# Attention on one core: the maxima subtracted once per block of queries, the weighted sums accumulated in the result's place

## The chip, the core and the metric

The kernel runs on one core of a Trainium2 chip. The metric is device time in microseconds (us): the median of three runs, and beside it one execution that the hardware profiler recorded. An instruction is named by its engine and its line in the kernel: TensorE (PE in the profile, its weight loads PEld), VectorE (DVE), ScalarE (ACT), GpSimd (POOL) and SyncE (SP).

## What is computed

Two layers run over x of shape (2, 256, 64, 64), all in fp32. The first is attention over the 4096 pixels with 8 heads of 32 channels, a projection and a residual:

```python
qkv = jnp.einsum('oc,bchw->bohw', w_qkv, x)
q, k, v = jnp.split(qkv, 3, axis=1)
scores = jnp.einsum('bhdi,bhdj->bhij', q, k) / jnp.sqrt(jnp.asarray(d, x.dtype))
attn = jax.nn.softmax(scores, axis=-1)
out = jnp.einsum('bhij,bhdj->bhdi', attn, v)
return jnp.einsum('oc,bchw->bohw', w_proj, out.reshape(b, c, h, w)) + x
```

The second is a non-local block: two 1x1 convolutions with bias and 2x2 max pooling (g of 256 channels, phi of 64), theta of 64 channels without pooling, a softmax over the 1024 pooled pixels for each of the 4096 pixels, a weighted sum, a 1x1 convolution W, a batch norm from given statistics, and a residual.

## The kernel before, in words

The heads are taken in groups of four, so that a group's 4 x 32 channels fill the 128 partitions. There are four groups (QUAD: two images, two groups each), and `n` is a group's number. A group's 4096 queries are cut into eight blocks of 512 (`i`), and for every block the 4096 keys are gone through in 32 steps of 128 keys (`j`, the loop in `attend`). A step computes the scores of 128 keys and 512 queries for four heads, in two pairs of heads, with keys on the partitions. ScalarE takes the exponential of a pair (L551) out of a PSUM tile of two banks, and one step later `weigh` (L435) multiplies the exponentials of the previous step with v, all four heads side by side in one PSUM buffer `w`. The 32 results of a block are added up in an SBUF tile `num`: ScalarE copies the first (L448), VectorE adds the others (L450).

The softmax subtracts each query's true maximum over all keys. The maxima are computed a block ahead by a second product with queries on the partitions (`product`, L264). The generator `maxima` is moved on twice in every step (`advance(maxes)`), so two of its products follow each pair's scores. The products of heads 0 and 1 are reduced by VectorE directly (`plain`, L276). Those of heads 2 and 3 mostly go in pairs of key chunks: a product with the difference of two chunks, cut off at zero by ScalarE (`pair`, L283), is added to the product with the first chunk while VectorE reduces it (`joint`, L290). For the first block of a new group, half of the chunks are plain for all heads (L330). All these products, `w`, the projections of q, k and v and the denominators use one ring of four PSUM buffers (`scratch`).

The maximum is subtracted by TensorE. `negate` splits the negated maxima into three bf16 terms on GpSimd, TensorE transposes them, and `subtract` (L424) writes them into a pair's PSUM tile by two bf16 matmuls with a matrix of ones (L427), ahead of the scores, which add to them. This is done in every fourth step. In the three steps after it the tile is kept: the score product takes the difference between the keys of this step and those of the last, so that the sum in PSUM becomes the next step's scores. To this end the order of the keys (`keys`, L400) goes by turns through four chunks of 512 keys: within each half of the keys, step j takes chunk j % 4. The differences of chunks are made by GpSimd and held in `kd` (chunks 1-0 and 3-2, two buffers by turns over groups), `last_kd` (5-4 and 7-6) and `mid_kd` (2-1 and 6-5). For the first group they are made as k is projected (in `make`). For later groups `differences` and `between` are called from `make` and from the loop of `attend`, at steps written out by hand (L561 to L567). `kd` and `last_kd` serve the maxima too.

The denominator is summed apart (`add`, L458): GpSimd adds up the exponentials of the first pair of heads over the steps 1 to 30 (L469), and DMAs that add in flight do it for the second pair (L477). `normalize` is a generator that is moved on during the next block: another such DMA (L483), the column sums by TensorE (L495), a reciprocal on a reshaped copy, and at last GpSimd's product of `num` and the reciprocal into the image's result tile `y` (L526).

While a block is worked on, at most three projections (the next group's k and v, this group's q of two blocks ahead; `during`, `make`) are placed after steps 11, 19 and 27. Within an engine the order of the instructions is that of the program, with a few pinned behind others (`issue_after`). After the two groups of an image come `project` and `non_local`. In `non_local`, the running sum of the exponentials (L706 to L711) uses the same two buffers as `num`; the tiles called `double` (five buffers) hold pairs of exponentials in attention and theta in `non_local`.

Of the kernel before, what the change touches and what calls it, by code (L numbers as in the profile page):

```python
# [9 lines left out]
F32 = mybir.dt.float32  # L10
# [6 lines left out]
N = HH * WW  # L17
# [5 lines left out]
P = 128  # L23
NC = C // P
NB = 512
NI = N // NB
NJ = N // P
# [8 lines left out]
def conv_attention(  # L36
# [131 lines left out]
    def make(what, n, i):  # L168
        b, qd = QUAD[n]
        if (b, i) not in held:  # L170
            name = f"x_{what}_{n}_{i}"
            if attending:
                held.clear()
                to = xs.tile([P, NC, NB], F32, tag="x", name=name)
            else:
                to = single(name)
            held[b, i] = load_x(b, i, to)
        xc = held[b, i]
        name = f"{what}_{b}_{qd}_{i}"
        pq = scratch(name)  # L180
        if what == "v":
            if i == 0:
                v[n] = qkv.tile([P, NJ, QH, D], F32, tag="v", name=f"v_{n}")
            for j in range(NB // P):
                for c in range(NC):
                    nc.tensor.matmul(  # L186
                        pq[:, bass.ts(j, P)],
                        xc[:, c, bass.ts(j, P)],
                        wv_sb[:, c, bass.ts(qd, P)],
                        start=(c == 0),  # L190
                        stop=(c == NC - 1),
                    )
                if j % 2 == 1:
                    yield
            nc.scalar.copy(v[n][:, bass.ts(i, NB // P)].rearrange("p j h d -> p (j h d)"), pq)
            return
        for c in range(NC):
            nc.tensor.matmul(  # L198
                pq,
                wqk_sb[:, c, qd, 0 if what == "q" else 1, :],  # L200
                xc[:, c, :],
                start=(c == 0),
                stop=(c == NC - 1),
            )
            yield
        if what == "q":
            to = q[n, i] = qkv.tile([P, NB], F32, tag="q", name=f"q_{n}_{i}", bufs=3)
        else:
            if i == 0:
                k[n] = qkv.tile([P, N], F32, tag="k", name=f"k_{n}")  # L210
            to = k[n][:, bass.ts(i, NB)]
        nc.scalar.copy(to, pq)
        if what == "k" and i % 4 == 2 and n == 0:
            between(n, i // 4)
        if what == "k" and i % 2 == 1 and n == 0:
            if i == 1:
                kd[n] = qkv.tile([P, NI // 4, NB], F32, tag="kd", name=f"kd_{n}")
            two = k[n][:, bass.ts(i // 2, 2 * NB)]
            nc.gpsimd.tensor_sub(  # L219
                (kd[n] if i < NI // 2 else last_kd)[:, i // 2 % (NI // 4), :],  # L220
                two[:, NB:],
                two[:, :NB],
            )
        elif what == "k" and i == NI // 2 - 1:
            kd[n] = qkv.tile([P, NI // 4, NB], F32, tag="kd", name=f"kd_{n}")
            differences(n, 0, kd[n])

    last_kd = const.tile([P, NI // 4, NB], F32, name="last_kd")  # L230

    def differences(n, half, to):
        two = k[n][:, bass.ts(half, N // 2)].rearrange("p (c t n) -> p c t n", t=2, n=NB)
        nc.gpsimd.tensor_sub(to, two[:, :, 1, :], two[:, :, 0, :])


    mid_kd = const.tile([P, 2, NB], F32, name="mid_kd")

    def between(n, half):
        two = k[n][:, N // 2 * half + NB :]  # L240
        nc.gpsimd.tensor_sub(mid_kd[:, half, :], two[:, NB : 2 * NB], two[:, :NB])

# [143 lines left out]
    def attend(b, y):  # L388
        class Block:


            def __init__(self, qd, i):
                self.n, self.qd, self.i = QUAD.index((b, qd)), qd, i
                self.name = f"{b}_{qd}_{i}"
                self.rows = self.n * NI + i
                self.num = None
                self.sums = {}
                self.last = []

        def keys(j):  # L400

            return j // 16 * 16 + j % 4 * 4 + j % 16 // 4

        def score(s, pair, blk, j):

            half, c, cols = j // 16, j % 4, bass.ts(j % 16 // 4, P)
            if c == 0:
                kj = k[blk.n][:, bass.ts(keys(j), P)]
            elif c == 2:
                kj = mid_kd[:, half, cols]  # L410
            else:
                kj = (last_kd if half else kd[blk.n])[:, c // 2, cols]
            for t in range(2):
                h = 2 * pair + t
                nc.tensor.matmul(  # L415
                    s[:, t, :],
                    kj[bass.ts(h, D), :],
                    q[blk.n, blk.i][bass.ts(h, D), :],
                    start=False,
                    stop=True,  # L420
                    skip_group_check=j % 4 > 0,
                )

        def subtract(s, pair, blk):  # L424
# [10 lines left out]
        def weigh(blk, j, p):  # L435

            w = scratch(f"w_{blk.name}_{j}")
            for h in range(QH):
                nc.tensor.matmul(  # L439
                    w[bass.ts(h, D), :],  # L440
                    v[blk.n][:, keys(j), h, :],
                    p[h // 2][:, h % 2, :],
                    start=True,
                    stop=True,
                )
            if j == 0:
                blk.num = work.tile([P, NB], F32, tag="num", name=f"num_{blk.name}")
                nc.scalar.copy(blk.num, w)  # L448
            else:
                nc.vector.tensor_add(blk.num, blk.num, w)  # L450

# [27 lines left out]
        def normalize(blk):  # L479
# [43 lines left out]
                for _ in range(13):  # L523
                    yield
            with tc.issue_after(added.ins):
                nc.gpsimd.tensor_mul(y[:, blk.qd, bass.ts(blk.i, NB)], blk.num, r)  # L526

        waiting, normal = None, iter(())
        for qd in range(QUADS):
            for i in range(NI):  # L530
                blk = Block(qd, i)
                items = [x for x in during(blk.n, i) if x[1] < len(QUAD)]
                both = [None, None]
                for j in range(NJ):
                    if j % 2 == 0:
                        two = double(f"p_{blk.name}_{j}_1")
                    p = [single(f"p_{blk.name}_{j}_0"), two[:, j % 2]]
                    for pair in (1, 0):
                        if j % 4 == 0:
                            s = both[pair] = scores(f"s_{blk.name}_{j}_{pair}")  # L540
                            subtract(s, pair, blk)
                            advance(maxes)
                            score(s, pair, blk, j)
                        else:
                            s = both[pair]
                            score(s, pair, blk, j)
                            advance(maxes)
                        with ExitStack() as order:
                            if cut is not None:
                                order.enter_context(tc.issue_after(cut.ins))  # L550
                            nc.scalar.activation(p[pair], s, AF.Exp, scale=scale)  # L551
                    if waiting is not None:
                        weigh(*waiting)
                        if j == 0:
                            normal = normalize(waiting[0])
                    add(blk, j, p, two)
                    waiting = blk, j, p
                    if j == 2 or j >= AFTER:
                        advance(normal)
                    if j % 2 == 0:  # L560
                        make_rows()  # L561
                        if (i, j) == (0, 2) and blk.n > 0:
                            between(blk.n, 1)
                        if (i, j) == (0, NJ // 4) and blk.n > 0:
                            differences(blk.n, 1, last_kd)
                        if (i, j) == (NI - 1, NJ // 2 + 2) and blk.n + 1 < len(QUAD):
                            between(blk.n + 1, 0)  # L567
                    elif j % 8 == 3 and j > 8 and items:
                        advance(make(*items.pop(0)), 9)
        weigh(*waiting)  # L570
# [26 lines left out]

    def non_local(b, y, theta_w, phi_w):
        theta = [double(f"theta_{b}_{t}") for t in range(2)]
        theta = [t[:, a, c, :] for t in theta for a in range(2) for c in range(2)]  # L600

        kv = qkv.tile([P, M + NC * M + M - 2 * P], F32, tag="k", name=f"kv_{b}")
# [100 lines left out]
        def weigh(i, t, p):  # L703
            if t == 0:
                acc[i] = [scratch(f"y_{b}_{i}_0"), scratch(f"y_{b}_{i}_1")]
                acc[i].append(work.tile([P, NB], F32, tag="num", name=f"sum1_{b}_{i}"))  # L706
                nc.gpsimd.tensor_add(acc[i][NC], p[:, 0, :], p[:, 1, :])
            else:

# [149 lines left out]
```

## Time and profile before

| | us |
|---|---|
| median of three runs (lowest, highest) | 3987.23 (3986.58, 3989.69) |
| the profiled execution, its time | 3986.37 |
| its span, first to last instruction | 3984.6 |
| TensorE busy | 3949.7 |
| VectorE busy | 2937.8 |
| GpSimd busy | 2903.6 |
| ScalarE busy | 2671.5 |
| attention of the first image, first to last weighing | 103.1 to about 1774 |
| attention of the second image | 2068.4 to about 3704 |
| exponentials L551: 2048 of | 1.025 |
| adds into num, L450: 992 of | 0.687 |
| first copies into num, L448: 32 of | 0.597 |
| adds of the first pair's exponentials, L469: 945 of | 2.460 |

TensorE's granted clock was 0.997 of full speed. A line of the costliest groups reads: line, engine, operation, output and inputs by the program's names, their shapes, how often; then the group's busy time in us and the mean of one in ns; then the idle time of the engine just before them and what ended it. A line of the timeline reads: start and duration in us, engine, line, operation, output and inputs, shapes, count, and in brackets the idle time before it with what released it. An fp32 matmul shows as two records.

### The profile page before, as it was taken

The page shows a single profiled execution, that of the slowest core. Times are in us where ns is not written, and L with a number is a line of the kernel's source. Part 1 is how long each engine was busy: PE and PEld are TensorE (multiplying, and loading weights), DVE is VectorE, ACT ScalarE, POOL GpSimd, SP SyncE. Part 2 cuts the span into 40 slices and gives each one's busy share as a digit, 9 for nine tenths or more (in the row PEclk, how much of TensorE's full clock was granted, in tenths as well). Part 3 has the DMA queues.
Part 4 walks back from the last instruction along what each step waited for, and adds up shares of the span by engine and source line. Part 5 has one row for each costly group of instructions (what it writes and reads, how often), then busy time and mean ns, then how long its engine had stood idle before and what let it go on. Part 6 is the DMA issues. An engine that isn't in the chain of part 4 may idle for free.

```text
span 3984.6 us, 72269 instructions
## 1 busy us (share of the span) xinstructions
PE 3949.7 (99%) x28592; PEld 1450.9 (36%) x28592; DVE 2937.8 (74%) x5451; ACT 2671.5 (67%) x3328; POOL 2903.6 (73%) x1851
## 2 busy tenths in 40 slices
PE   8999999999999999999999999999999999999998
PEld 4333333333333333333333333333333333333333
DVE  5877877788777787774457877787888888884434
ACT  4777777777777777751137777777677777777121
POOL 1888888888888888871448888888888888886043
PEclk9999999999999999999999999999999999999999
DMA  1777877887777777880017788878787778778200
GB/s 56 146 160 165 166 165 164 170 166 163 165 162 164 163 165 164 170 198 8 22 39 163 165 166 166 173 165 170 162 173 164 164 165 166 163 163 182 66 16 27
DMA packets 113941, 569.56 MB, mean 143 GB/s; under 512 B 20296, under 2 KB 22600, under 8 KB 52416
## 3 DMA queue, kind: packets, MB, share of 16 engines
q0 software_dynamic: 68832, 501.25, 62.8%
q1 hardware_dynamic: 44080, 62.88, 4.5%
q8 instruction: 224, 3.67, 0.4%
q14 instruction: 117, 0.96, 0.1%
q10 hardware_dynamic: 688, 0.79, 0.1%
HBM read 54.78 MB, written 8.88 MB: 16 GB/s over the span
## 4 chain that ended last, share of the span: by engine, by line
PE 97%; DVE 2%; DMA 0%; ACT 0%; POOL 0%; issue 0%; DVEq 0%; ACTq 0%
PE w L439 26%; PE ps L264 26%; PE s L415 24%; PE y L715 6%; PE s L427 3%; PE q L198 2%; PE v L186 2%; PE k L198 2%; PE den L495 1%; PE g L640 1%; DVE r L729 1%; PE f L683 1%; PE proj L584 1%; PE f L749 1%; PE tp L624 0%; PE tp L620 0%
## 5 line engine op out<-in xcount | busy, mean ns | idle before, releaser
L469 POOL TENSOR_TENSOR p<-p,p 128x1024 f32<-128x1024 f32 x945 | 2324.7, 2460 | 557.0 <-ACT p L551 550.1
L551 ACT ACTIVATE p<-s 128x1024 f32<-128x1024 f32 x2048 | 2089.9, 1025 | 624.1 <-PE ps L264 408.5
L264 PE MATMUL ps<-k,q 32*128 32x512 f32 x6232 | 2049.0, 627 | 4.0 <-DVE part L276 1.7
L276 DVE TENSOR_REDUCE part<-ps 128x1 f32<-128x512 f32 x2136 | 1369.9, 686 | 574.2 <-PE ps L264 557.7
L439 PE MATMUL w<-p,v 128*32 128x512 f32 x8192 | 1091.0, 605 | 0.7 <-ACT p L551 0.7
L450 DVE TENSOR_TENSOR num<-num,w 128x512 f32<-128x512 f32 x992 | 681.4, 687 | 92.7 <-PE w L439 91.3
L290 DVE CUSTOM_DVE_ANT_0 ps<-ps,over 128x512 f32<-128x512 f32 x980 | 676.0, 693 | 32.1 <-PE ps L264 27.9
L264 PEld LDWEIGHTS ps<-k,q 32*128 32x128 f32 x6232 | 636.5, 183 | 55.7 <-DVE num L450 8.7
L283 ACT ACTIVATE over<-ps 128x512 f32<-128x512 f32 x916 | 543.2, 593 | 15.2 <-PE ps L264 14.0
L264 PE MATMUL ps<-kd,q 32*128 32x512 f32 x1056 | 518.2, 595 | 0.7 <-POOL kd L219 0.7
L415 PE MATMUL s<-q,k 32*128 32x512 f32 x2048 | 513.2, 590 | 0.0
L415 PE MATMUL s<-q,kd 32*128 32x512 f32 x2048 | 511.1, 616 | 0.4 <-ACT p L551 0.3
L415 PE MATMUL s<-q,mid_kd 32*128 32x512 f32 x2048 | 510.1, 614 | 0.0
L415 PE MATMUL s<-q,last_kd 32*128 32x512 f32 x2048 | 506.8, 614 | 0.0
L439 PEld LDWEIGHTS w<-p,v 128*32 128x32 f32 x8192 | 161.1, 108 | 799.0 <-DVE part L276 769.4
L264 PE MATMUL ps<-last_kd,q 32*128 32x512 f32 x904 | 437.4, 590 | 1.5 <-POOL last_kd L219 1.5
L477 POOL DMA_DIRECT2D p<-p x448 | 395.5, 883 | 33.4 <-ACT p L551 28.7
L415 PEld LDWEIGHTS s<-q,mid_kd 32*128 32x128 f32 x2048 | 173.0, 183 | 309.7 <-ACT over L283 197.1
L415 PEld LDWEIGHTS s<-q,kd 32*128 32x128 f32 x2048 | 174.6, 184 | 282.2 <-ACT over L283 177.8
L415 PEld LDWEIGHTS s<-q,last_kd 32*128 32x128 f32 x2048 | 173.1, 183 | 269.6 <-ACT over L283 164.3
L715 PE MATMUL y<-p,kv 128*128 128x512 f32 x512 | 240.0, 608 | 6.4 <-DVE r L729 6.4
L764 ACT ACTIVATE p<-f 128x1024 f32<-128x1024 f32 x64 | 65.6, 1025 | 248.4 <-PE f L749 219.1
(108 smaller groups left out, 2720.4 us busy)
## 6 DMA issues: line engine op xcount, KB each, us to landing
p<-p POOLq DMA_DIRECT2D x478, 1024.0 KB, 7.5
x_k<-in_x_dram SPq DMA_DIRECT2D x32, 512.0 KB
x_q<-in_x_dram SPq DMA_DIRECT2D x30, 512.0 KB
x_res<-in_x_dram SPq DMA_DIRECT2D x16, 512.0 KB
out_dram<-z SPq DMA_DIRECT2D x16, 512.0 KB
r<-flat SPq DMA_DIRECT2D x120, 64.0 KB
x_v<-in_x_dram SPq DMA_DIRECT2D x6, 512.0 KB
wqk_sb<-in_wqk_dram ACTq DMA_DIRECT2D x1, 512.0 KB
```

The costliest lines, as they stand in the source:

```text
L198: nc.tensor.matmul(pq, wqk_sb[:, c, qd, 0 if what == "q" else 1, :], xc[:, c, :], start=(c == 0), stop=(c == NC - 1),)
L264: nc.tensor.matmul(ps, q[n, i][bass.ts(h, D), bass.ts(g, P)], keys[bass.ts(h, D), :], start=True, stop=True,)
L276: reduced = nc.vector.tensor_reduce(part[:, g, h, j : j + 1], ps, AX.X, ALU.max)
L283: cut = nc.scalar.activation(over, ps, AF.Relu)
L290: reduced = nc.vector.tensor_tensor_reduce(out=ps, in0=ps, in1=over, scale=1.0, scalar=LEAST, op0=ALU.add, op1=ALU.max, accum_out=part[:, ...
L415: nc.tensor.matmul(s[:, t, :], kj[bass.ts(h, D), :], q[blk.n, blk.i][bass.ts(h, D), :], start=False, stop=True, skip_group_check=j % 4 > 0,)
L439: nc.tensor.matmul(w[bass.ts(h, D), :], v[blk.n][:, keys(j), h, :], p[h // 2][:, h % 2, :], start=True, stop=True,)
L450: nc.vector.tensor_add(blk.num, blk.num, w)
L469: added = nc.gpsimd.tensor_add(blk.sums[0], blk.sums[0], p[0])
L477: nc.gpsimd.dma_start(out=blk.sums[n], in_=two, accum_op=ALU.add)
L551: nc.scalar.activation(p[pair], s, AF.Exp, scale=scale)
L715: nc.tensor.matmul(acc[i][o], wg[:, 2 * t + j, bass.ts(o, P)], p[:, j, :], **edge)
```

## The change

The subtraction is done in step 0 of a block only, and the PSUM tiles of both pairs are kept for all 32 steps. The keys now go by turns through all eight chunks: step j takes chunk j % 8. `mid_kd` therefore holds three differences (2-1, 4-3, 6-5), and a new tile `turn_kd` holds the step from chunk 7 back to chunk 0 at the next 128 keys, made by the new function `rounds`. In the steps that used to subtract, the scores now stand ahead of the maxima's products, as in the others. For groups after the first, a new function `renew` makes the differences around the change of groups: at steps 26, 28 and 30 of the group's last block and steps 0 and 2 of the next group's first. `kd` is made in two instructions in place of one. A block's `num` is its slice of `y`: VectorE copies the first weighted sum there and adds the others, and GpSimd's product works in place. In `non_local` the running sum moves to four buffers in a tile of the `double` kind.

```diff
--- before.py
+++ after.py
@@ -210,35 +210,57 @@
                 k[n] = qkv.tile([P, N], F32, tag="k", name=f"k_{n}")
             to = k[n][:, bass.ts(i, NB)]
         nc.scalar.copy(to, pq)
-        if what == "k" and i % 4 == 2 and n == 0:
-            between(n, i // 4)
+        if what == "k" and i % 2 == 0 and i > 0 and n == 0:
+            between(n, i // 2 - 1)
+        if what == "k" and i == NI - 1 and n == 0:
+            rounds(n)
         if what == "k" and i % 2 == 1 and n == 0:
             if i == 1:
                 kd[n] = qkv.tile([P, NI // 4, NB], F32, tag="kd", name=f"kd_{n}")
-            two = k[n][:, bass.ts(i // 2, 2 * NB)]
-            nc.gpsimd.tensor_sub(
-                (kd[n] if i < NI // 2 else last_kd)[:, i // 2 % (NI // 4), :],
-                two[:, NB:],
-                two[:, :NB],
-            )
+            differences(n, i // 2, (kd[n] if i < NI // 2 else last_kd)[:, i // 2 % (NI // 4), :])
         elif what == "k" and i == NI // 2 - 1:
             kd[n] = qkv.tile([P, NI // 4, NB], F32, tag="kd", name=f"kd_{n}")
-            differences(n, 0, kd[n])
+            for c in range(2):
+                differences(n, c, kd[n][:, c, :])
 
 
 
     last_kd = const.tile([P, NI // 4, NB], F32, name="last_kd")
 
-    def differences(n, half, to):
-        two = k[n][:, bass.ts(half, N // 2)].rearrange("p (c t n) -> p c t n", t=2, n=NB)
-        nc.gpsimd.tensor_sub(to, two[:, :, 1, :], two[:, :, 0, :])
-
-
-    mid_kd = const.tile([P, 2, NB], F32, name="mid_kd")
-
-    def between(n, half):
-        two = k[n][:, N // 2 * half + NB :]
-        nc.gpsimd.tensor_sub(mid_kd[:, half, :], two[:, NB : 2 * NB], two[:, :NB])
+    def differences(n, c, to):
+        two = k[n][:, bass.ts(c, 2 * NB)]
+        nc.gpsimd.tensor_sub(to, two[:, NB:], two[:, :NB])
+
+
+
+    mid_kd = const.tile([P, NI // 2 - 1, NB], F32, name="mid_kd")
+    turn_kd = const.tile([P, NB // P - 1, P], F32, name="turn_kd")
+
+    def between(n, c):
+        two = k[n][:, NB * (2 * c + 1) : NB * (2 * c + 3)]
+        nc.gpsimd.tensor_sub(mid_kd[:, c, :], two[:, NB:], two[:, :NB])
+
+    def rounds(n):
+        nc.gpsimd.tensor_sub(
+            turn_kd,
+            k[n][:, P:NB].rearrange("p (a n) -> p a n", n=P),
+            k[n][:, N - NB : N - P].rearrange("p (a n) -> p a n", n=P),
+        )
+
+    def renew(i, j, n):
+
+
+        if (i, j) == (NI - 1, NJ - 6):
+            between(n + 1, 0)
+        elif (i, j) == (NI - 1, NJ - 4):
+            between(n + 1, 1)
+        elif (i, j) == (NI - 1, NJ - 2):
+            differences(n + 1, 2, last_kd[:, 0, :])
+            between(n + 1, 2)
+        elif (i, j) == (0, 0):
+            differences(n, 3, last_kd[:, 1, :])
+        elif (i, j) == (0, 2):
+            rounds(n)
 
 
 
@@ -393,23 +415,25 @@
                 self.n, self.qd, self.i = QUAD.index((b, qd)), qd, i
                 self.name = f"{b}_{qd}_{i}"
                 self.rows = self.n * NI + i
-                self.num = None
+                self.num = y[:, qd, bass.ts(i, NB)]
                 self.sums = {}
                 self.last = []
 
         def keys(j):
 
-            return j // 16 * 16 + j % 4 * 4 + j % 16 // 4
+            return j % NI * (NB // P) + j // NI
 
         def score(s, pair, blk, j):
 
-            half, c, cols = j // 16, j % 4, bass.ts(j % 16 // 4, P)
-            if c == 0:
-                kj = k[blk.n][:, bass.ts(keys(j), P)]
-            elif c == 2:
-                kj = mid_kd[:, half, cols]
+            c, a = j % NI, j // NI
+            if j == 0:
+                kj = k[blk.n][:, :P]
+            elif c == 0:
+                kj = turn_kd[:, a - 1, :]
             else:
-                kj = (last_kd if half else kd[blk.n])[:, c // 2, cols]
+                made = mid_kd if c % 2 == 0 else kd[blk.n] if c < NI // 2 else last_kd
+                at = c // 2 - 1 if c % 2 == 0 else c // 2 % 2
+                kj = made[:, at, bass.ts(a, P)]
             for t in range(2):
                 h = 2 * pair + t
                 nc.tensor.matmul(
@@ -418,7 +442,7 @@
                     q[blk.n, blk.i][bass.ts(h, D), :],
                     start=False,
                     stop=True,
-                    skip_group_check=j % 4 > 0,
+                    skip_group_check=j > 0,
                 )
 
         def subtract(s, pair, blk):
@@ -444,8 +468,7 @@
                     stop=True,
                 )
             if j == 0:
-                blk.num = work.tile([P, NB], F32, tag="num", name=f"num_{blk.name}")
-                nc.scalar.copy(blk.num, w)
+                nc.vector.tensor_copy(blk.num, w)
             else:
                 nc.vector.tensor_add(blk.num, blk.num, w)
 
@@ -523,7 +546,7 @@
                 for _ in range(13):
                     yield
             with tc.issue_after(added.ins):
-                nc.gpsimd.tensor_mul(y[:, blk.qd, bass.ts(blk.i, NB)], blk.num, r)
+                nc.gpsimd.tensor_mul(blk.num, blk.num, r)
 
         waiting, normal = None, iter(())
         for qd in range(QUADS):
@@ -536,7 +559,7 @@
                         two = double(f"p_{blk.name}_{j}_1")
                     p = [single(f"p_{blk.name}_{j}_0"), two[:, j % 2]]
                     for pair in (1, 0):
-                        if j % 4 == 0:
+                        if j == 0:
                             s = both[pair] = scores(f"s_{blk.name}_{j}_{pair}")
                             subtract(s, pair, blk)
                             advance(maxes)
@@ -559,12 +582,9 @@
                         advance(normal)
                     if j % 2 == 0:
                         make_rows()
-                        if (i, j) == (0, 2) and blk.n > 0:
-                            between(blk.n, 1)
-                        if (i, j) == (0, NJ // 4) and blk.n > 0:
-                            differences(blk.n, 1, last_kd)
-                        if (i, j) == (NI - 1, NJ // 2 + 2) and blk.n + 1 < len(QUAD):
-                            between(blk.n + 1, 0)
+                        if i > 0 and blk.n + 1 < len(QUAD) or i == 0 and blk.n > 0:
+                            with tc.issue_after(added.ins) if added else ExitStack():
+                                renew(i, j, blk.n)
                     elif j % 8 == 3 and j > 8 and items:
                         advance(make(*items.pop(0)), 9)
         weigh(*waiting)
@@ -597,6 +617,7 @@
 
     def non_local(b, y, theta_w, phi_w):
         theta = [double(f"theta_{b}_{t}") for t in range(2)]
+        sums = double(f"sums1_{b}")
         theta = [t[:, a, c, :] for t in theta for a in range(2) for c in range(2)]
 
         kv = qkv.tile([P, M + NC * M + M - 2 * P], F32, tag="k", name=f"kv_{b}")
@@ -703,7 +724,7 @@
         def weigh(i, t, p):
             if t == 0:
                 acc[i] = [scratch(f"y_{b}_{i}_0"), scratch(f"y_{b}_{i}_1")]
-                acc[i].append(work.tile([P, NB], F32, tag="num", name=f"sum1_{b}_{i}"))
+                acc[i].append(sums[:, i // 2 % 2, i % 2, :])
                 nc.gpsimd.tensor_add(acc[i][NC], p[:, 0, :], p[:, 1, :])
             else:
 
```

## The prediction

> **What bounds the kernel now.** I read the page first: its engine line, then the chain.
>
> ```profile
> PE 3949.7 (99%) x28592; PEld 1450.9 (36%) x28592; DVE 2937.8 (74%) x5451; ACT 2671.5 (67%) x3328; POOL 2903.6 (73%) x1851
> ...
> PE 97%; DVE 2%; DMA 0%; ACT 0%; POOL 0%; issue 0%; DVEq 0%; ACTq 0%
> PE w L439 26%; PE ps L264 26%; PE s L415 24%; PE y L715 6%; PE s L427 3%; PE q L198 2%; PE v L186 2%; PE k L198 2%; PE den L495 1%; PE g L640 1%; DVE r L729 1%; PE f L683 1%; PE proj L584 1%; PE f L749 1%; PE tp L624 0%; PE tp L620 0%
> ```
>
> TensorE is on the path for 97% of the span. The subtraction of the maxima (L427) has 3% of the chain, about 120 us, which the change cuts to an eighth. That share must not be taken as the price: matmuls overlap, so I went on to the timeline of TensorE's instructions and measured a step from the start of one L439 group (weighing) to the start of the next. One subtracting step and the start of its neighbours:
>
> ```profile
> 799.70 0.39 PE L427 MATMUL s<-rows,ones_b 32*128 32x512 bf16 x2
> 799.70 0.70 PE L264 MATMUL ps<-k,q 32*128 32x512 f32 x2
> 799.92 0.59 PE L415 MATMUL s<-q,k 32*128 32x512 f32 x2
> ...
> 800.66 0.38 PE L427 MATMUL s<-rows,ones_b 32*128 32x512 bf16 x2
> ...
> 801.83 1.07 PE L439 MATMUL w<-p,v 128*32 128x512 f32 x8
> 802.83 0.70 PE L415 MATMUL s<-q,last_kd 32*128 32x512 f32 x2
> 802.84 0.70 PE L264 MATMUL ps<-k,q 32*128 32x512 f32 x2
> ...
> 804.79 1.07 PE L439 MATMUL w<-p,v 128*32 128x512 f32 x8
> 805.79 0.70 PE L415 MATMUL s<-q,mid_kd 32*128 32x512 f32 x2
> ```
>
> The first columns are start and duration. The subtracting step lasts 802.83 - 799.70 = 3.13 us, the next 805.79 - 802.83 = 2.96. The first L427 pair costs almost nothing: it runs beside maxima products on other row groups, and the second half step begins 0.96 us in, just as without it (0.97: 803.80 against 802.83). Only the second pair pushes the weighing back, to 2.13 us after the step's start, against 1.96 (804.79 - 802.83). Going through all 1024 steps of the timeline this way: 176 with a subtraction and nothing else have a median of 3.134 us, 706 plain ones 2.959. **The price of a subtracting step is 0.175 us.**
>
> The first step of a block is a separate case. Its plain steps 1 to 2 (weighing to weighing) take 3.22 us in 31 blocks, though nothing is subtracted there; a block that starts at 1044:
>
> ```profile
> 1045.68 0.60 ACT L448 COPY num<-w 128x512 f32<-128x512 f32 x1
> ...
> 1046.33 0.69 PE L264 MATMUL ps<-k,q 32*128 32x512 f32 x1
> 1046.37 1.29 DVE L276 TENSOR_REDUCE part<-ps 128x1 f32<-128x512 f32 x2 [1.00 <-PE ps L264]
> ...
> 1047.38 1.07 PE L439 MATMUL w<-p,v 128*32 128x512 f32 x8
> ```
>
> The weighed sum w sits in the ring of four PSUM buffers that the maxima products use too. ScalarE's copy queues behind an exponential and ends at 1046.28; the product that gets w's buffer starts at 1046.33, 0.2 us behind its partner. The weighing before was at 1044.16, so this step took 3.22 us.
>
> [...] here durations of about 600 ns stand beside starts 430 ns apart. [...] L427 and L264 both start at 799.70. [...] The score follows its subtraction by 0.22 us[...]. [...] no copy of this shape on VectorE is in the trace, and the nearest row, the 128x512 add of L450, takes 687. I take 687.
>
> **The change, part by part.**
> Removed: seven of eight subtractions per block, 32 blocks.
> - 28 ordinary blocks: 28 x 7 x 0.175 = 34.3 us. The 78 such steps that also hold a q, k or v projection are counted too: they take 5.05 (q, k) or 5.12 us, that is 3.134 plus 1.91 or 1.98, so the same price is in them.
> - Three blocks (those in which the maxima of a new group of heads run ahead on half the keys in plain form, L330; starts 831.8, 1670.7, 2797.1) have steps of 3.06 to 3.33 us from the twelfth on, subtracting or not: VectorE has four reductions of 0.645 and an add of 0.69 there, about 3.27 us. Two of the seven subtractions are free there and two stand beside a projection, which I count half: 3 x 4 x 0.175 = 2.1 us.
> - The last block has no maxima; its subtracting steps take 3.02 against 2.90: 7 x 0.12 = 0.8 us.
> Together 37.2 us. Bounds: nothing for steps with a projection gives 24; more than 0.175 per step is excluded, as the plain step exists 706 times at 2.959.
>
> Order within those steps: score now stands ahead of the maxima products, as in the 706 plain steps. It waits for the exponential of the step before, as the subtraction did; behind it on TensorE wait maxima, the other pair and the weighing. No new wait.
>
> First sum by VectorE: it takes the slot that the add L450 has in every other step, and ScalarE loses 0.6 us where it was late. An ordinary add ends 1.82 us after the weighing (703.43 to 705.25), 0.14 before the product that needs the buffer (1.96). With 687 ns or less the 3.22 falls to 2.96: 31 x 0.265 = 8.2 us, and 29 follow-on steps at 2.997 lose 0.037: 1.1. Together 9.3 us; bounds 0 (the copy late after all) and 9.3.
>
> Sums in y: the same adds (L450, 992 of 687 ns) to another address; the product L526 in place. Price 0. It needs tracking by region: y is written by two engines. Already k is filled in slices while others are read: L264 starts on the first half of last_kd at 64.75, its second half is written at 68.53.
>
> Differences on GpSimd, per group of heads: before two mid_kd (1.41), one kd (2.60), one last_kd (2.80), 8.2 us; after seven of 1.27 to 1.41 and one of 384 columns, an estimate of 0.95 from 1.27 for 512 and 2.60 for 1024; about 10.4. Five fall at the group's change, 26th step to 2nd: 6.5 us. They cut in on GpSimd's queue ahead of the adds L469, the accumulating DMAs L477 and, for the last, behind DMA L483. Cover: steps 31 and 0 add nothing.
>
> ```profile
> 1045.89 2.36 POOL L469 TENSOR_TENSOR p<-p,p 128x1024 f32<-128x1024 f32 x1 [6.17 <-ACT p L551]
> ```
>
> That idle 6.17 us, the 0.47 us per two steps before the even adds and the projection in step 28 hold them. Their users, scores at steps 2 to 8, come five or six steps (15 us) later, and the first operand's six buffers allow as much. Price 0; without that cover 6.5 us at three changes, 20 us.
> At the start the new turn_kd stands on GpSimd ahead of the last difference, for which TensorE already waits 0.75 us (69.85). **Plus 1.0 us.**
>
> Second layer: its running sum moves to four buffers in another pool; adds L711 wait for ScalarE (110 us), not for buffers. Price 0. No DMA is added, and SyncE's queue is untouched.
>
> Sum: -37.2 - 9.3 + 1.0 = -45.5 us. The profiled execution took 3986.4 us (span 3984.6 and 1.8 around it), 0.9 under the median of 3987.2: 3940.9 or 3941.7. **I say 3941.**
>
> **Rivals.**
> A: the copy frees the buffer too late on VectorE, so the stall stays. For: the margin is 0.14 us. Against: it only replaces an add of the same shape. 3987 - 36 = 3951.
> B: GpSimd falls behind at the group changes, and scores or exponentials wait: 20 us back, 3961. For: it is busy 82% of a stretch of attention (163.8 of 200 us). Against: the 6.17 us.
> C, slower: each add into y waits for GpSimd's product into another slice of y, because y counts as one tile. Once per block an add then stands behind what GpSimd has before that product: an add of 2.46 and the product of 1.44, less 0.14 of margin, some 3.8 us, and TensorE stands with the ring full. 30 x 3.8 = 113 us: 3987 - 45 + 113 = 4055. It decides from 1.5 us per block on (45.5 / 30). Against: the slices of last_kd.
> D: L427's whole share of the chain goes: 7/8 of 120 = 105, 3987 - 114 = 3873. Against: plain steps are already at 2.959.
>
> **How the numbers follow.** Forecast 0.81 (3932 to 3947), A 0.07, B 0.06, C 0.04, D 0.02. The range reaches from 3932 to A's 3954 and leaves out B, C, D and a little. Within 0.2% of 3987 (about 8 us, what a measurement here can tell from nothing) lies only C at a part of its price: 0.02, of C's and B's chances. Slower 0.03, the rest of C. Faster 0.95.
>
> **What would show it.** L427 at 128 matmuls; steps 4, 8, 24 of an ordinary block at 2.96 us, the first at 2.96; ordinary blocks at 104.25 - 1.23 - 0.30 = 102.7 us; the three VectorE-bound ones 1.0 shorter; no score waiting for turn_kd, mid_kd or last_kd. I am wrong if plain steps grow above 2.96, or VectorE's adds wait for GpSimd.

## The result and the profile after

| | before | after |
|---|---|---|
| median, us (lowest to highest) | 3987.04 (3986.58 to 3989.69) | 3948.49 (3945.67 to 3950.00) |
| profiled execution, us | 3986.37 | 3947.82 |
| its span | 3984.6 | 3945.3 |

The ratio is 0.9901, 95% interval 0.9886 to 0.9915: 38.6 us less. The forecast was 3941, so 7.5 us of the expected gain are missing. The page of the changed kernel has the same shape as before. Its engine line and its chain:

```profile
PE 3906.9 (99%) x27696; PEld 1378.1 (35%) x27696; DVE 2936.6 (74%) x5483; ACT 2654.9 (67%) x3296; POOL 2909.0 (74%) x1865
...
PE 97%; DVE 2%; DMA 1%; ACT 0%; POOL 0%; issue 0%; DVEq 0%; ACTq 0%; POOLq 0%
PE s L439 28%; PE w L463 26%; PE ps L286 23%; PE y L736 6%; PE q L198 2%; PE v L186 2%; PE k L198 2%; PE den L518 2%; PE g L661 1%; DVE r L750 1%; PE f L704 1%; PE proj L604 1%; PE f L770 1%; PE tp L645 0%; PE tp L641 0%; DMA x_res<-in_x_dr
```

TensorE has 28592 - 27696 = 896 matmuls fewer, 28 per block, and the subtraction has left the chain. The chain's 3% did not turn into 105 us: the share of the scores rose from 24% to 28%, that of the maxima's products fell from 26% to 23%, and every other line's stayed within a point. TensorE's timeline around a step in which the kernel before subtracted (step 8 of a block; scores are now L439, maxima L286, weighing L463):

```profile
535.88 0.70 PE L439 MATMUL s<-q,turn_kd 32*128 32x512 f32 x2
535.89 0.70 PE L286 MATMUL ps<-k,q 32*128 32x512 f32 x2
...
537.84 1.06 PE L463 MATMUL w<-p,v 128*32 128x512 f32 x8
538.83 0.70 PE L439 MATMUL s<-q,kd 32*128 32x512 f32 x2
538.85 0.70 PE L286 MATMUL ps<-k,q 32*128 32x512 f32 x2
...
540.80 1.07 PE L463 MATMUL w<-p,v 128*32 128x512 f32 x8
541.79 0.70 PE L439 MATMUL s<-q,mid_kd 32*128 32x512 f32 x2
```

From score to score it lasts 538.83 - 535.88 = 2.95 us, the next 2.96; before they were 3.13 and 2.96. The scores from turn_kd wait for nothing here. The beginning of a block, VectorE and TensorE in the timeline:

```profile
1035.08 1.06 PE L463 MATMUL w<-p,v 128*32 128x512 f32 x8
...
1036.24 0.69 DVE L471 COPY y<-w 128x512 f32<-128x512 f32 x1
...
1037.05 0.63 PE L286 MATMUL ps<-k,q 32*128 32x512 f32 x1
...
1037.30 1.29 DVE L298 TENSOR_REDUCE part<-ps 128x1 f32<-128x512 f32 x2 [0.36 <-PE ps L286]
...
1038.04 1.07 PE L463 MATMUL w<-p,v 128*32 128x512 f32 x8
```

VectorE frees the buffer at 1036.93, 0.12 us before the product that takes it, and the step is 1038.04 - 1035.08 = 2.96 us in place of 3.22. The copy takes 0.692.

Summed over the two stretches of attention, first weighing to last of an image, the gain in these two profiles is (1671.4 + 1622.7) - (1649.6 + 1600.6) = 43.9 us. (Before, the last weighing of the second image is at 3691.1 us, not at the 3704 of the table ahead.) Ordinary blocks went from 104.25 to 102.71. But the first weighing came at 106.2 in place of 103.1, and the last one is followed by 295.1 us in place of 293.5.

### The profile page after: what moved, and what is told of

It reads as the page before. It is cut to its first block, busy times and chain, and to the rows that moved or that the text cites. A ratio compares the mean times of both kernels' runs of the same rounds, so it can differ in the third digit from the quotient of the medians.

```text
span 3945.3 us, 70296 instructions
## 1 busy us (share of the span) xinstructions
PE 3906.9 (99%) x27696; PEld 1378.1 (35%) x27696; DVE 2936.6 (74%) x5483; ACT 2654.9 (67%) x3296; POOL 2909.0 (74%) x1865
## 4 chain that ended last, share of the span: by engine, by line
PE 97%; DVE 2%; DMA 1%; ACT 0%; POOL 0%; issue 0%; DVEq 0%; ACTq 0%; POOLq 0%
PE s L439 28%; PE w L463 26%; PE ps L286 23%; PE y L736 6%; PE q L198 2%; PE v L186 2%; PE k L198 2%; PE den L518 2%; PE g L661 1%; DVE r L750 1%; PE f L704 1%; PE proj L604 1%; PE f L770 1%; PE tp L645 0%; PE tp L641 0%; DMA x_res<-in_x_dram 0%
## 5 line engine op out<-in xcount | busy, mean ns | idle before, releaser
L286 PE MATMUL ps<-k,q 32*128 32x512 f32 x6232 | 2017.1, 628 | 4.0 <-DVE part L298 1.7
L463 PE MATMUL w<-p,v 128*32 128x512 f32 x8192 | 1091.0, 605 | 0.6 <-ACT p L574 0.6
L439 PE MATMUL s<-q,mid_kd 32*128 32x512 f32 x3072 | 767.0, 614 | 0.0
L473 DVE TENSOR_TENSOR y<-y,w 128x512 f32<-128x512 f32 x992 | 679.2, 685 | 57.4 <-PE w L463 57.2
L286 PEld LDWEIGHTS ps<-k,q 32*128 32x128 f32 x6232 | 629.0, 183 | 42.6 <-DVE part L298 8.6
L286 PE MATMUL ps<-kd,q 32*128 32x512 f32 x1056 | 519.4, 596 | 0.7 <-POOL kd L232 0.7
L439 PE MATMUL s<-q,kd 32*128 32x512 f32 x2048 | 512.2, 616 | 0.4 <-ACT p L574 0.4
L439 PE MATMUL s<-q,last_kd 32*128 32x512 f32 x2048 | 508.7, 614 | 0.0
L463 PEld LDWEIGHTS w<-p,v 128*32 128x32 f32 x8192 | 161.1, 108 | 804.8 <-DVE part L298 775.2
L286 PE MATMUL ps<-last_kd,q 32*128 32x512 f32 x904 | 437.4, 590 | 2.4 <-POOL last_kd L232 2.4
L439 PEld LDWEIGHTS s<-q,mid_kd 32*128 32x128 f32 x3072 | 261.8, 183 | 413.7 <-ACT over L305 226.4
L439 PEld LDWEIGHTS s<-q,kd 32*128 32x128 f32 x2048 | 177.6, 184 | 306.6 <-ACT over L305 195.4
L439 PEld LDWEIGHTS s<-q,last_kd 32*128 32x128 f32 x2048 | 176.6, 183 | 265.2 <-ACT over L305 143.4
L732 POOL TENSOR_TENSOR sums<-sums,p 128x512 f32<-128x512 f32 x96 | 121.4, 1264 | 114.3 <-ACT p L785 110.5
```

Source lines behind the costliest of these rows:

```text
L286: nc.tensor.matmul(ps, q[n, i][bass.ts(h, D), bass.ts(g, P)], keys[bass.ts(h, D), :], start=True, stop=True,)
L439: nc.tensor.matmul(s[:, t, :], kj[bass.ts(h, D), :], q[blk.n, blk.i][bass.ts(h, D), :], start=False, stop=True, skip_group_check=j > 0,)
L463: nc.tensor.matmul(w[bass.ts(h, D), :], v[blk.n][:, keys(j), h, :], p[h // 2][:, h % 2, :], start=True, stop=True,)
```

## The experiments

Theory: TensorE's row groups (heads 0 and 1 use one half of its rows, heads 2 and 3 the other) set the step, a subtraction costs 0.175 us per step and the late copy 0.3 us per block; what is missing lies outside the plain steps. Rivals: the copy and the subtraction share a gain; the place of the sums costs something; the loss at the start is one of load times alone. The runs were taken on three chips; beside them the kernel before had medians of 3987.92, 3986.92 and 3987.97.

**The changed kernel again**, as the base of a series on one chip.

> The changed kernel once more, as the base for the others of this series on the same chip: 3948 us (3945 to 3951). If the 7 us that it lies above my 3941 were chance of the load times at the start and between the images, its lowest runs should come near 3943; if they are a fixed loss, none will fall below 3945.

Measured: 3948.53 (3946.14 to 3950.15). None of the four fell below 3945, so a fixed loss is likely.

**turn_kd made last at the start.**

```diff
-        if what == "k" and i == NI - 1 and n == 0:
-            rounds(n)
...
             differences(n, i // 2, (kd[n] if i < NI // 2 else last_kd)[:, i // 2 % (NI // 4), :])
+            if i == NI - 1:
+                rounds(n)
```

> The changed kernel with the difference turn_kd made after the last last_kd in place of ahead of it. My theory: TensorE's wait for last_kd at the start falls from 1.69 to 0.75 us, so 0.9 us less than the changed kernel. Rival: the 3.1 us by which the first weighing came later in the changed kernel's trace hang on this wait as a whole (through the slow clock after it), then 2 to 3 us less.

Measured: 3945.14 (3944.28 to 3945.87), 3.4 us less than the base, with no overlap between the runs. The wait before the last difference's first product, in the changed kernel:

```profile
69.61 0.99 POOL L244 TENSOR_TENSOR turn_kd<-k 128x384 f32<-128x384 f32 x1 [3.00 <-ACT k L212]
70.56 1.26 POOL L232 TENSOR_TENSOR last_kd<-k 128x512 f32<-128x512 f32 x1
71.88 1.14 PE L286 MATMUL ps<-last_kd,q 32*128 32x512 f32 x8 [1.69 <-POOL last_kd L232]
...
106.21 1.07 PE L463 MATMUL w<-p,v 128*32 128x512 f32 x8
```

and in this one:

```profile
69.83 1.27 POOL L232 TENSOR_TENSOR last_kd<-k 128x512 f32<-128x512 f32 x1 [3.00 <-ACT k L212]
71.05 1.00 POOL L244 TENSOR_TENSOR turn_kd<-k 128x384 f32<-128x384 f32 x1
71.15 1.14 PE L286 MATMUL ps<-last_kd,q 32*128 32x512 f32 x8 [0.75 <-POOL last_kd L232]
...
104.39 1.06 PE L463 MATMUL w<-p,v 128*32 128x512 f32 x8
```

The brackets give the idle time: the change had added 0.94 us, as forecast. The 3.4 us of the medians are nearer to the rival's 2 to 3 than to the theory's 0.9. TensorE's first instruction waited for the DMA of wqk_sb and came at 5.8 to 6.7 us, differently from profile to profile, so I count from GpSimd's first line above, which starts when k is there, to the first weighing (L463). That is 104.39 - 69.83 = 34.56 us here, and 36.60 and 37.17 in the two profiles of the changed kernel. The kernel before has 34.57; the kernel before with its sums in y, an experiment further down, has the short wait too (0.74), but takes 35.66. First the kernel before, then that one, two lines of the timeline and one of the stretches each (stretch, its length, TensorE's busy us and count, its granted clock, DMA share and GB/s):

```profile
68.53 1.27 POOL L219 TENSOR_TENSOR last_kd<-k 128x512 f32<-128x512 f32 x1 [2.99 <-ACT k L212]
98.00:101.00 3.00, 2.90 (x23) 0.84 0.02 5
103.10 1.07 PE L439 MATMUL w<-p,v 128*32 128x512 f32 x8
```

```profile
68.16 1.27 POOL L219 TENSOR_TENSOR last_kd<-k 128x512 f32<-128x512 f32 x1 [3.00 <-ACT k L212]
98.00:101.00 3.00, 3.00 (x20) 0.50 0.03 5
103.82 1.06 PE L439 MATMUL w<-p,v 128*32 128x512 f32 x8
```

What differs is the clock. TensorE runs at half of it (0.50) for 10.2 us in the kernel before and in this one (88.7 to 99.0, 90.8 to 101.0), but for 13.7 us with the sums in y (87.8 to 101.5) and in the changed kernel (90.0 to 103.7; in its second profile 3.4 us from 73.2 on and 10.2 from 93.6 on). So the longer stretch at half clock costs 1.1 us (34.57 to 35.66), and the longer wait costs the 0.94 us that it lasts (35.66 to 36.60). All six profiles with the long wait have 13.7 us at half clock, but so have two of the five with the short one. In three of the six a part of 3.4 us begins within 1.4 us of the long wait's end. That the wait brings the longer stretch, as the rival says, is thus likely for these three and not shown for the others.

**Only the copy moved.** In the kernel before:

```diff
-                nc.scalar.copy(blk.num, w)
+                nc.vector.tensor_copy(blk.num, w)
```

> The kernel before with only the first copy of a block moved from ScalarE to VectorE, num kept. My theory: the steps 1 to 2 of a block fall from 3.22 to 2.96 us and the next from 3.00 to 2.96, so 3987 - 9.3 = 3978. Rival: VectorE frees the buffer as late as ScalarE did, no difference, 3987.

Measured: 3980.71 against 3987.92, ratio 0.9982 (0.9975 to 0.9988): 7.2 us less. The step came down to 3.025 us (median), not 2.96. So neither the theory nor the rival (VectorE as late as ScalarE) is right as it stands: VectorE is late, but by less. Its timeline in this kernel at a block's beginning:

```profile
1043.57 0.14 DVE L290 DVE_READ_ACCUMULATOR2_ANT part<- 128x1 f32 x1
1043.73 0.69 DVE L448 COPY num<-w 128x512 f32<-128x512 f32 x1
```

The copy starts 0.16 us after the start of the instruction ahead of it, where the one into y in the changed kernel starts after 0.09 (1036.15, 1036.24). The line of the copy has 29 extra EVENT_SEMAPHORE instructions on VectorE (0.021 each) in this kernel and none where the copy goes into y. A likely reason is that num has two buffers used by turns, so that its first writer must also wait for GpSimd's product of an earlier block. The copy starts 0.07 us later and the step lasts 0.066 us longer, so almost nothing of the 0.12 us between the copy's end and the product was margin: in both kernels the next weight load for the maxima follows the copy's end by 0.06 us (1044.42 and 1044.48 here, 1036.93 and 1036.99 in the changed one).

**The copy back on ScalarE**, in the changed kernel (into y):

```diff
-                nc.vector.tensor_copy(blk.num, w)
+                nc.scalar.copy(blk.num, w)
```

> The changed kernel with the first copy of a block on ScalarE again (into y). My theory: the two parts add, so it gives the 9.3 us back: 3948 + 9 = 3957. Rival: without the subtractions ScalarE has less time per step and the copy costs more, up to 0.6 us per block, 3948 + 19 = 3967; or the stall came from the subtraction in the next step and is gone, 3948.

Measured: 3954.83 against 3948.53, 6.3 us more where 9.3 were expected. The first steps are at 3.224 us again, so the stall does not come from the subtraction. The step after stays at 2.96, so 1.1 of the 9.3 us were not to be had. All first steps together take 8.1 us more, attention as a whole 6.5 to 6.9 (against the two profiles of the changed kernel): the two parts add only roughly.

**The copy moved and the sums in y**, in the kernel before: the line above, `self.num = y[:, qd, bass.ts(i, NB)]`, no buffer num in attention, and GpSimd's product in place.

> The kernel before with the copy on VectorE and the sums in y, but the subtraction in every fourth step and the old order of keys. My theory: the place of the sums costs nothing, the same as with the copy alone, 3978. Rival C of the prediction in a small form: adds into y wait for GpSimd's product at another slice, up to 1 us per block, 3978 + 30 = 4008.

Measured: 3979.65 against 3986.92, ratio 0.9981 (0.9974 to 0.9989): 7.3 us less. The first steps are at 2.959 now, which gives an ordinary block another 0.07 us (104.02 to 103.95); that is too little for the medians to show. The copy starts 0.09 us after the start of the instruction ahead, and its line has no EVENT_SEMAPHORE, which fits the reason given above. The image tile that two engines write caused no wait; my forecast C has fallen.

**Empty subtractions.** The changed kernel with bf16 matmuls of zeros in front of the maxima's products in steps 4, 8, 12 and so on. They add nothing to the scores. In the loop over `pair in (1, 0)`, with PAIRS as (1,), (0,) or (0, 1):

```diff
+                        elif j % 4 == 0 and pair in PAIRS:
+                            s = both[pair]
+                            nothing(s, pair)
+                            advance(maxes)
+                            score(s, pair, blk, j)
```

> The changed kernel, with two bf16 matmuls of ones and zeros (they add nothing) ahead of the maxima's products in steps 4, 8, 12 ... of a block, in the first half step only (heads 2 and 3). As I read it in the prediction, the first pair of a subtracting step costs almost nothing: 3948 to 3951. The rival: each pair of heads has its own row groups, and each row group carries one bf16 pass more than before, so that one pair alone costs as much as both: 0.15 to 0.175 us in some 200 steps, 3948 + 30 to 39 = 3978 to 3987.

> The same with the two empty matmuls in the second half step only (heads 0 and 1). As I read it in the prediction, this pair is the one that costs: 3948 + 36 = 3984. The rival (row groups in parallel) says the same, 3978 to 3987; if the two pairs share the cost, both kernels lie at 3966.

> The same with the empty matmuls in both half steps, which is the work of the old subtraction in the new order of keys. Both theories: 3948 + 36 = 3984. If the order of keys or the place of the sums mattered by itself, this would not come back to the kernel before less the 9.3 us of the copy, 3978 to 3984.

Measured: first pair alone 3963.4, second alone 3983.71, both 3984.1, against 3948.5 without. Per step (median) that is 3.033, 3.141 and 3.134 us against 2.958: 0.075, 0.183 and 0.176. The second pair alone and both came within 1 us of the 3984 expected. Neither expectation for the first pair holds, neither free nor at full price. TensorE's timeline of one step with the first pair alone (zeros are L464, scores L441, maxima L288, weighing L477):

```profile
538.56 0.39 PE L464 MATMUL s<-zeros_b,ones_b 32*128 32x512 bf16 x2
538.56 0.70 PE L288 MATMUL ps<-k,q 32*128 32x512 f32 x2
...
539.64 0.59 PE L288 MATMUL ps<-kd,q 32*128 32x512 f32 x1
...
540.59 1.06 PE L477 MATMUL w<-p,v 128*32 128x512 f32 x8
```

and with both:

```profile
540.90 0.39 PE L464 MATMUL s<-zeros_b,ones_b 32*128 32x512 bf16 x2
...
541.87 0.38 PE L464 MATMUL s<-zeros_b,ones_b 32*128 32x512 bf16 x2
541.98 0.59 PE L288 MATMUL ps<-kd,q 32*128 32x512 f32 x1
...
542.08 0.59 PE L441 MATMUL s<-q,turn_kd 32*128 32x512 f32 x2
...
543.03 1.06 PE L477 MATMUL w<-p,v 128*32 128x512 f32 x8
```

Heads 2 and 3 and heads 0 and 1 use different row groups, and their first products start together (538.56 in the first kernel, 540.90 in the second). Each of the two has its own row of work: heads 2 and 3 first their scores, then their maxima's products, heads 0 and 1 the other way round. In the first kernel the row of heads 2 and 3 is late: its second product starts 1.08 us into the step (plain: 0.96), and the weighing comes at 2.03. In the second the row of heads 0 and 1 carries the zeros too: its scores start at 1.18 (plain 0.97) and the weighing comes at 2.13. The weighing waits for the later row, so the first pair's lateness is covered by the second's. All three medians fit that the later of two rows sets the step: 2.96 + 0.075, + 0.18, and the larger of the two for both. In the steps with zeros the scores also stand behind the maxima's products, as in the kernel before; that order without zeros was not run.

With both pairs, an ordinary block takes 103.95 us, as in the kernel before with the copy moved and the sums in y, so the new order of the keys costs nothing there. The median is 4.5 us above that kernel's. The longer wait at the start is 0.94 of it. In the profile (3987.82, among the slowest of its twelve runs) three single steps in the first blocks of groups take 4.0 to 4.3 us in place of 2.96; what they wait for was not pursued.

**Pairs of chunks for every block's maxima.** The changed kernel with turn_kd made last, last_kd in two buffers by turns and five buffers (six before) for the first pair's exponentials:

```diff
-        chunks = 0 if h < 2 else NI // 2 if i == 0 and n > 0 else NI
+        chunks = 0 if h < 2 else NI
...
+        elif what == "k" and i == NI - 1:
+            last_kd[n] = qkv.tile([P, NI // 4, NB], F32, tag="lkd", name=f"lkd_{n}")
+            for c in range(2):
+                differences(n, 2 + c, last_kd[n][:, c, :])
```

> The changed kernel with turn_kd made last at the start, last_kd in two buffers by turns (made while the last chunk of k is projected), and the maxima of every block taken in pairs of chunks, those of a new group's first block too; one buffer fewer for the first pair's exponentials (five) makes room. My theory: the subtractions removed from the three blocks bound by VectorE gave nothing because VectorE set the step there (3.2 us); with pairs those steps fall to 2.96: about 16 steps x 0.24 x 3 = 12 us less than the changed kernel, 3936. Rival: those steps are set by TensorE's order or the ring of four buffers, then no gain, 3947; or five buffers are too few and exponentials wait for GpSimd, slower than 3948.

Measured: 3932.58 (3931.60 to 3933.80), ratio to the kernel before 0.9863 (0.9847 to 0.9880). That is below both kernels: 15.9 us under the changed one and 12.6 under the one with only turn_kd moved. Busy times in 44 us of one of the three blocks bound by VectorE (columns: stretch, its length, then busy us and count for TensorE, its weight loads, VectorE, ScalarE, GpSimd, then clock, DMA share and GB/s), in the changed kernel:

```profile
862.00:906.00 44.00, 44.00 (x332) 19.53 (x328) 40.04 (x69) 26.92 (x28) 36.04 (x20) 1.00 0.86 182
```

and with pairs throughout:

```profile
860.00:904.00 44.00, 44.00 (x360) 15.53 (x360) 36.56 (x74) 35.18 (x44) 38.30 (x21) 1.00 0.89 187
```

TensorE reads 44.00 us busy in both, yet it issued 332 matmuls in the first and 360 in the second. VectorE fell from 91% to 83% busy, and ScalarE took over a part of its work. The steps went from alternating 2.99 and 3.41 us to 2.96, and each of the three blocks lost 3.97 us: 11.9 together, as expected. The rest of the 15.9 is about what moving turn_kd gave. A step has as many matmuls in both, so it was not TensorE's own work that set the step there. The expectation that the removed subtractions "gave nothing" there was too low: these blocks fell from 107.81 us (the kernel before with the copy moved and the sums in y) to 107.44. So VectorE set the step there, as the theory has it.

## Why the prediction was right and where it was off

The time lies in the range, and the mechanism held: an ordinary block takes 103.95 us with the copy and the sums moved and 102.71 with the subtractions gone too, 1.24 us for seven steps, where seven times the price of 0.175, read from start-to-start distances, is 1.23. The price by the chain's share (forecast D) was wrong by almost three times: 105 us, against 35.9 in attention between the two kernels. The late copy was real, and it does not come from the subtraction.

The number alone would not have shown this. With 3948.5 us the median lies outside the forecast's own 3932 to 3947 and nearer to rival A's 3951 than to 3941; it is in the range because the range reaches as far as A. But A's stall is gone in the changed kernel (the first steps have a median of 2.959 us, none above 3.1). The 7.5 us are missing for other reasons, and it is luck that they did not add up to more. A came true in small with num kept: there the copy still frees the buffer 0.066 us late.

One reading was right in its sum and not in its parts: the first pair of a subtracting step "costs almost nothing" only behind the second. Alone it costs 0.075 us; the second costs 0.18 with it or without. A score follows its subtraction by 0.22 us, so two pairs one behind the other would have cost 0.44 by my estimate, and more than half of that was hidden.

What was mis-sized, with 43.9 us in attention where I had 46.5:
- "28 ordinary blocks": in seven blocks of the last group the step with the keys 28 has no projection and takes 3.84 us before and 3.90 after. VectorE makes the next block's maximum ready there (L358, 0.28 us), and TensorE waits 0.42 us for the add (L450) behind it. With the copy and the sums moved and the subtraction kept the step takes 3.91, so the subtraction was free. These blocks gained 1.2 to 1.4 us, not 1.53: 1.6 us less in all.
- "Two stand beside a projection, which I count half", and the copy: the three VectorE-bound blocks gained 0.70 us each, not 1.0: 0.9 us.

The first copy's 9.3 us came in the changed kernel, but not from the copy alone. Summed over all blocks, the first two steps lost 7.4 us with the copy alone and 9.6 with the sums in y too (the medians of these kernels fell by 7.2 and 7.3). The price of the copy, 0.687 from the add of the same shape, was right (0.692). The margin of 0.14 us was not safe: 0.07 us more on VectorE lengthened the step by 0.066 as long as num was a buffer of its own. "Price 0" for the sums in y was right as to waiting for another slice, but missed that they spare this delay.

What was too small: "plus 1.0 us" at the start. The wait grew by 0.94 us as worked out, but from k to the first weighing it lasts 2.0 to 2.6 us longer. The rest, 1.1 to 1.7 us, goes with 3.4 us more of half clock. TensorE's clock is not in the prediction's sum at all. Moving turn_kd behind the difference gave 2.0 us back there and 3.4 us in the medians; the 1.4 between them is not explained.

What stays open: the profiled executions gained 38.6 us where 45.5 were forecast. Of the 6.9 missing, 2.6 lie in attention, 1.0 between k and the first weighing, 1.1 ahead of k (68.53 against 69.61; TensorE's first instruction came 0.9 later), 1.6 behind the last weighing and 0.7 outside the span; 0.2 were gained between the images. The last four differ from profile to profile, whatever the kernel, and in part with the clock: between the two images' attention lie 292.4 us in the two profiles without half clock there and 293.4 to 294.0 in the six with 6.8 us of it; after the last weighing 297.2 to 298.3 in the four with 3.4 us of half clock within 15 us of it and 292.6 to 295.8 in the other seven. Why the stretches at half clock differ was not tested.

The slower forecast C did not occur, nor B: GpSimd still has 6.16 us idle at the start of a block, and the scores from turn_kd waited 0.8 us once in the changed kernel's profile.

## What to carry to other kernels

Take the price of a matmul from the difference between steps with it and without it. Here two row groups of TensorE worked side by side, and only the later one counted (0.075 us for the first pair alone, 0.18 for the second alone and for both); the share of the chain (105 us against 35.9) and the sum of durations (0.39 + 0.38 us for the two pairs of L427 against 0.175) overstated the price. Where another engine frees a buffer of a ring just ahead of its next use, look at every such place: here a gap of 0.12 us in the timeline was no margin. And the gain on TensorE was worth little in the blocks where VectorE set the step (0.70 us, against 104.25 - 102.71 = 1.54 in an ordinary one), so go through the blocks one by one before multiplying by their number.

## What the runs showed of the hardware that was not expected

A bf16 pair ahead of fp32 matmuls on its own row groups cost less than its length: 0.22 us of work (the scores start that much behind it) moved the second product of these rows by 0.12 us (0.96 to 1.08). The second pair, in the middle of the step, moved its rows by 0.21 (0.97 to 1.18). In plain steps the first fp32 product of a step is followed by the next after 0.53 us and later ones after 0.43; with the bf16 pair ahead, the scores follow each other after 0.43 from the start. At the start TensorE ran at half clock for 10.2 us in three of the eleven profiles and for 13.7 in eight, and the 3.4 us more cost 1.1 us up to the first weighing with the same wait (34.57 and 35.66).
